# The first image of a convolution and attention kernel: channels normalised half by half, tables loaded later

## The chip, the cores and the metric

The kernel runs on one core of a Trainium2 chip. The metric is the device time of one execution in microseconds (us); lower is better. A kernel's time is the median of its runs.

## What is computed

The reference takes an image batch x of shape (2, 256, 56, 56) through a convolutional layer and one layer of two parts behind it. What matters here is the first layer, and in front of it a normalisation over groups of eight channels:

```
x = group_norm(x)                        # groups of 8 channels, per image
y = einsum('oc,bchw->bohw', w_qkv1, x)   # 256 -> 768 channels
y = depthwise_conv3x3(y, w_qkv2)         # 9 taps per channel
q, k, v = y.reshape(B, H, W, 3, 8, 32)   # a reshape of the flat array
for s in (0, 1):                         # two neighbourhood attentions, 7 x 7, dilation 1 and 2
    attn = softmax(q k + bias table of rpb[s]);  out = attn v
o = einsum('oc,bchw->bohw', w_proj, out)
```

Then a linear attention with a feed-forward part and a mixture of eight experts with two chosen per token follow. Everything is in 32-bit floats.

## The kernel before, in words

**Start.** The class `Convolutions` (L419) loads the whole image x_sb as [128, 2, 3136]: the 256 channels are two halves of 128 partitions (ct = 0 and 1). `load_x` (L462) issues four transfers for each half, ct 0 on SyncE's queue and ct 1 on ScalarE's. Then come g8 (the matrix that averages over eight channels), w2 (the taps), wq1 (the 256 x 768 weights, on SyncE's queue). `norm_image` (L469) takes 14 statistics on VectorE (seven chunks of 448 columns, two halves), two aggregates, a matmul with g8 for the mean, four small operations, a matmul for the variance, a power on GpSimd, and then scales x_sb in place in six operations, both halves in turn, chunk by chunk. Which instruction comes first on an engine is decided by a scheduler from the order of the program and from priorities; `tc.issue_after(x)` holds an instruction behind another one, `tc.high_priority()` moves it ahead, and `tc.manual_schedule(engines=...)` keeps the written order on those engines.

**Convolution.** `run` (L504) goes over two images, six blocks of 128 output channels (oc) and two strips of 28 rows (hf). For each strip, four groups of rows (8, 8, 8 and 5) are multiplied (L529, two channel halves accumulated in one PSUM bank, two banks in turn), copied by ScalarE into the padded strip ypad (L535), and put through nine taps: TensorE does the first 8 rows with diagonal matrices (L550), which GpSimd makes from w2 (diag, L519); ScalarE does the first tap of the other 20 rows (yc, L569) and VectorE the other eight (L579). The strip is stored to HBM (yd, L587). There are two ypad strips and two yc buffers.

**Bias tables.** `bias_tables` (L363) builds for each of the two attentions a table of exponentials. pf is zeroed (L368) and written to HBM as frame (L371); the 676 values of rpb are written reversed, one by one, to turned in HBM (L374); turned is written into frame (L379), frame is read back into pf (L383). After the first two strips, ScalarE takes the exponential (L387), GpSimd multiplies with a column mask (cm, L405) and with the two columns of far (L407 to L409), and stores three tables fp per attention (L411). The attention loads table tiles from fp (L714).

**Queues.** SyncE issues nearly all transfers in its own order: x, weights, frame and turned, the stores of yd, the table tiles, and the loads of q, k and v from yd (L804, L863). An instruction that waits holds up what stands behind it. Eight semaphores serve the transfers of both queues in turn, so that a transfer waits for the eighth before it.

**Attention and later stages.** `first_image` (L1064) runs the convolution and the first image's attention side by side: `conv.run()` and `att.run()` are generators that are stepped in turn. `Attention` (L607) holds PSUM tiles s_ps (four banks) and po (two banks) and loads the projection weights wpr (L639) when it is made. In the linear part, `keys` (L267) reads the tokens t, normalises them, rescales them (L296) and adds the output bias b2 if it was given one (L300); for the first half of the tokens it was given none but for the shared block t_ab, and `message` (L1918) adds it on GpSimd (L1925).

Of the kernel before, what the change touches and what calls it, by code (L numbers as in the profile page):

```python
# [13 lines left out]
F32 = mybir.dt.float32  # L14
AF = mybir.ActivationFunctionType
ALU = mybir.AluOpType
# [4 lines left out]
P = 128  # L21
B, C, HH, WW = 2, 256, 56, 56
T = HH * WW
# [3 lines left out]
G = 448  # L27
NG = T // G
NA = -(-T // 128)
NH6 = (NA - 1) // 4  # L30
NH = 4
# [95 lines left out]
def hybrid_kernel(ctx: ExitStack, tc: tile.TileContext, a: dict, out: bass.AP):  # L127
    nc = tc.nc
# [138 lines left out]
    def keys(tk, wk, sm, ps, bank, w_k, b2, kx, acc, n0, n, p, first, last, eager):  # L267
# [27 lines left out]
        for k in range(n):  # L295
            nc.scalar.activation(  # L296
                t[:, k, :], t[:, k, :], AF.Identity, bias=up[:, 1, k : k + 1], scale=up[:, 0, k : k + 1]
            )
        if b2 is not None:
            nc.gpsimd.tensor_tensor(t, t, b2[p].unsqueeze(1).to_broadcast([rows, n, C]), ALU.add)  # L300
        yield
        kps = bank()[p]
        for k in range(n):
# [59 lines left out]
    def bias_tables(sp, ac, pp):  # L363

        held = []
        for s in range(2):
            pf = sp.tile([NH * 21, 33], F32, name=f"pf{s}", bufs=1)
            nc.vector.memset(pf, 0.0)  # L368
            rpb = a[f"L0_conv_rpb{s}"]
            frame = dram.tile([NH, 21, 33], F32, name=f"frame{s}")  # L370
            nc.sync.dma_start(frame.rearrange("h r c -> (h r) c"), pf)  # L371
            turned = dram.tile([NH * 13, 13], F32, name=f"turned{s}")
            with nc.allow_non_contiguous_dma(reason="676 values"):
                nc.sync.dma_start(  # L374
                    turned, bass.AP(rpb.tensor, rpb.offset + 12, [[13, NH * 13], [-1, 13], [1, 1]])
                )
            held.append((pf, frame, turned))
        for pf, frame, turned in held:
            nc.sync.dma_start(  # L379
                frame[:, 4:17, 10:23],  # L380
                bass.AP(turned.tensor, turned.offset + 156, [[169, NH], [-13, 13], [1, 13]]),
            )
            nc.sync.dma_start(pf, frame.rearrange("h r c -> (h r) c"))  # L383
        yield
        for s in range(2):
            nw, pf = wide[s], held[s][0]
            nc.scalar.activation(pf, pf, AF.Exp)  # L387
            far = sp.tile([NH * 21, 2], F32, name=f"far{s}", bufs=1)
            nc.sync.dma_start(far, a["c_far"])

            if s == 0:
                stage = [ac.tile([P, 2, 800], F32, name="acc1") for _ in range(2)]
            else:
                stage = [
                    pp.tile([TT, NH, 448], F32, name="p").rearrange("p h n -> p (h n)")
                    .rearrange("p (k n) -> p k n", k=2) for _ in range(2)
                ]
            cm, near, late, early = (
                stage[k // 2][: NH * 21, k % 2, : KC * nw].rearrange("p (c j) -> p c j", j=nw) for k in range(4)
            )  # L400
            nc.sync.dma_start(cm, a[f"c_cm{s}k"].rearrange("p (c j) -> p c j", j=nw))
            o = 0
            for j0, nj in cols_of[s]:
                seen = bass.AP(pf.tensor, pf.offset + j0, [pf.ap[0], [1, KC], [1, nj]])
                nc.gpsimd.tensor_tensor(cm[:, :, o : o + nj], cm[:, :, o : o + nj], seen, ALU.mult)  # L405
                o += nj
            nc.gpsimd.tensor_scalar(late, cm, far[:, 0:1], 1.0, ALU.mult, ALU.mult)  # L407
            nc.gpsimd.tensor_scalar(early, cm, far[:, 1:2], 1.0, ALU.mult, ALU.mult)
            nc.gpsimd.tensor_scalar(near, late, far[:, 1:2], 1.0, ALU.mult, ALU.mult)  # L409
            for f, t in zip(fp[s], (near, late, early)):  # L410
                nc.gpsimd.dma_start(  # L411
                    bass.AP(
                        f.tensor, f.offset + (KC - 1) * NH * 21 * nw,
                        [[nw, NH * 21], [-NH * 21 * nw, KC], [1, nw]],
                    ),
                    t,
                )

    class Convolutions:  # L419


        def __init__(self, ctx):
# [11 lines left out]
            for hf in range(2):  # L434
                nc.gpsimd.memset(self.ypads[hf][:, hf * (HH // 2 + 1), :], 0.0)
                nc.gpsimd.memset(self.ypads[hf][:, :, 0:1], 0.0)
                nc.gpsimd.memset(self.ypads[hf][:, :, WW + 1 : WW + 2], 0.0)
            self.load_x(0)
            self.g8 = self.cw.tile([P, P], F32, name="g8")
            nc.scalar.dma_start(self.g8, a["c_g8"])  # L440
            self.w2 = self.cw.tile([P, 6, 9], F32, name="w2")
            nc.scalar.dma_start(
                self.w2, a["L0_conv_w_qkv2"].rearrange("(oc p) one kh kw -> p oc (one kh kw)", p=P)
            )
            self.wq1 = self.cw.tile([P, 2, 3 * C], F32, name="wq1")
            nc.sync.dma_start(self.wq1, a["w_qkv1_t"].rearrange("(ct p) o -> p ct o", p=P))

        def share(self, ctx):

# [51 lines left out]
                        gm[:, ct : ct + 1], grs[:, ct : ct + 1], ALU.subtract, ALU.mult,  # L501
                    )

        def run(self):  # L504


            w2 = self.w2
            for _ in self.norm_image():
                pass
            yield 0, 0  # L510
            for b, oc in ((b, oc) for b in range(B) for oc in range(6)):
                diag = None
                for hf in range(2):
# [8 lines left out]

                    r0 = hf * HH // 2
                    ypad = self.ypads[hf]
                    q0 = r0 - hf
                    for g0, n in ((0, 8), (8, 8), (16, 8), (24, 5)):
                        py = self.bank([P, 8, WW], "py")
                        for ct in range(2):
                            nc.tensor.matmul(  # L529
                                py[:, :n, :], self.wq1[:, ct, oc * P : (oc + 1) * P],  # L530
                                self.x_sb[:, ct, (q0 + g0) * WW : (q0 + g0 + n) * WW],
                                start=(ct == 0), stop=(ct == 1),
                            )
                        k0 = 1 - hf + g0
                        anchors["copied"] = nc.scalar.copy(  # L535
                            ypad[:, k0 : k0 + n, 1 : WW + 1], py[:, :n, :]
                        ).ins
                        if not shared:
                            yield b, oc
# [67 lines left out]
    class Attention:  # L607
# [6 lines left out]
        def __init__(self, ctx, b, order, banks=None, spare=None):  # L614
# [8 lines left out]
            self.ps_s = ctx.enter_context(tc.tile_pool(name=f"p2ps{b}", bufs=1, space=PSUM, **kw))  # L623
            bp, op = self.pool["b"], self.pool["x"]
            self.wpr = op.tile([P, 2, C], F32, name="wpr", bufs=1)
            if not banks:
                self.load_projection()
            self.ones = op.tile([TT, HD], F32, name="ones2", bufs=1)
            nc.vector.memset(self.ones, 1.0)
            self.qT0 = bp.tile([P, HH, WW], F32, name="qT0")  # L630
# [433 lines left out]
    def first_image(conv, ph):  # L1064
# [2 lines left out]
        ctx = ExitStack()  # L1067
        att = Attention(ctx, 0, "l k b t p v r x ac")
        conv.share(ctx)
        run, steps = conv.run(), att.run()  # L1070
        need = next(steps)
        tables = bias_tables(conv.sp, att.pool["ac"], att.pool["p"])
        next(tables)
        for k, (b, done) in enumerate(run):
            if k == 5:
                with tc.issue_after(anchors["copied"]):
                    next(tables, None)
# [581 lines left out]
    def linear(ph, tk, half, behind=None):  # L1659
# [258 lines left out]
        def message(n0, n, qz, out):  # L1918
# [1 line left out]
            mns = []  # L1920
            ss = sm.tile([P, 4], F32, name="ssm")
            for k0 in range(0, n, 2):
                if half == 0:
                    tt = tk.at(n0 + k0, 2)
                    nc.gpsimd.tensor_tensor(tt, tt, b2.unsqueeze(1).to_broadcast([P, 2, C]), ALU.add)  # L1925
                pm = ps_h.tile([P, 2, C], F32, name="pm", tag="h")
                for k in range(min(2, n - k0)):
                    for b, c0, c1 in parts(n0, n):
# [204 lines left out]
        def all_keys():  # L2133
# [6 lines left out]
            for i in range(len(pairs) + 2):  # L2140
                for k in (1, 0, 2):
                    j = i - k
                    if j == i and j < len(pairs):
                        live[j] = keys(
                            tk, wk, sm, ps_a, bank, w_k, b2 if half or pairs[j][1] == 1 else None, kx, acc, *pairs[j], j == 0, j == len(pairs) - 1, j < 3 and half == 0
                        )
                    if 0 <= j < len(pairs):
                        next(live[j])
# [325 lines left out]
```

## Time and profile before

| | us |
|---|---|
| median of three runs | 1997.98 |
| lowest and highest run | 1995.13, 2001.15 |
| the profiled execution, its time | 1985.54 |
| its span in the trace | 1983.8 |
| first product matmul starts | 18.49 |
| first tap on VectorE starts | 28.41 |
| VectorE resumes after its longest stop of the first 100 us | 73.46 |

The profile shows one execution, which was faster than the runs that the median is of; durations in it are compared with its own time. The span is the time from the first to the last instruction, and 1.74 us lie around it. In a timeline, a line gives the start, the time covered, the engine (PE is TensorE, PEld its weight loads, DVE VectorE, ACT ScalarE, POOL GpSimd, SP SyncE; a q behind it is the engine's own queue), the line of the kernel, the operation, the tile written and the tile read, how often it runs in a row, and in brackets how long the engine was idle before it and what ended that. A line of waits names who waited and for whom, then the total in us, the number of waits and the longest. A matmul of 32-bit floats leaves two records.

### The profile page before, as it was taken

How to read it: one execution, taken by the hardware profiler on the slowest of the kernel's cores; microseconds unless marked ns; L12 is line 12 of the kernel's file. 1: busy time of each engine (PE TensorE's matmuls, PEld its weight loads, DVE VectorE, ACT ScalarE, POOL GpSimd, SP SyncE). 2: the span in 40 equal slices, each digit the busy share in tenths (PEclk: the TensorE clock that was granted, in tenths of full speed). 3: DMA queues.
4: the chain of work that ended last, by engine and by line, in shares of the span. 5: the costliest groups of instructions: out<-in, count | busy, mean ns of one | idle time of the engine just before them, and what ended most of it. 6: DMA issues, size and time to landing. Idle time of an engine off the chain costs nothing.

```text
span 1983.8 us, 27692 instructions
## 1 busy us (share of the span) xinstructions
PE 1840.1 (93%) x9996; PEld 1304.7 (66%) x9996; DVE 1093.3 (55%) x2728; ACT 705.8 (36%) x1337; POOL 578.8 (29%) x634
## 2 busy tenths in 40 slices
PE   6999899988989997999989989999999999999996
PEld 3444454556645564665668755668788888888885
DVE  6887988889888546555557434655622222222121
ACT  2233324334434223544536543323322222222332
POOL 4520042025202444111126311345422323222221
PEclk9999999999989996999999999999999999999998
DMA  4644422350003334754464210114677676767995
GB/s 113 152 114 128 152 75 84 101 151 35 25 33 94 107 85 140 205 153 137 130 191 126 72 35 32 46 62 133 182 227 198 185 201 186 200 190 197 299 279 166
DMA packets 200147, 268.79 MB, mean 135 GB/s; under 512 B 30952, under 2 KB 158614, under 8 KB 199760
## 3 DMA queue, kind: packets, MB, share of 16 engines
q1 hardware_dynamic: 167920, 223.95, 37.4%
q0 software_dynamic: 19728, 27.54, 7.4%
q10 hardware_dynamic: 12352, 15.43, 2.3%
q8 instruction: 81, 1.33, 0.3%
q14 instruction: 66, 0.54, 0.1%
HBM read 200.19 MB, written 70.95 MB: 137 GB/s over the span
## 4 chain that ended last, share of the span: by engine, by line
PE 48%; DMA 5%; DVE 3%; ACT 3%; issue 1%; SPq 0%; POOL 0%; ACTq 0%; DVEq 0%; POOLq 0%
PE ph L1617 13%; PE py L1637 13%; PE p L1961 4%; DMA xr<-xs 2%; PE x L1637 2%; PE py L1977 2%; PE x L1617 2%; DMA xs<-in_c_fill 2%; PE po L666 2%; PE pm L1931 1%; PE kx L317 1%; PE x L359 1%; PE kp L305 1%; PE pq L1888 1%; PE px L1584 1%; PE s_ps L652 1%
## 5 line engine op out<-in xcount | busy, mean ns | idle before, releaser
L1617 PE MATMUL ph<-xe,w1e 128*128 128x256 f32 (+1 forms) x1448 | 309.2, 369 | 10.6 <-ACT hT L1621 4.1
L1637 PE MATMUL py<-w2e,hT 128*128 128x256 f32 x1392 | 311.3, 379 | 0.0
L1621 ACT ACTIVATE hT<-ph,sv 128x256 f32<-128x256 f32 (+1 forms) x362 | 165.7, 462 | 387.3 <-PE ph L1617 384.2
L1617 PEld LDWEIGHTS ph<-xe,w1e 128*128 128x128 f32 x1448 | 261.2, 190 | 49.8 <-ACT hT L1621 6.1
L1637 PEld LDWEIGHTS py<-w2e,hT 128*128 128x128 f32 x1392 | 260.1, 190 | 33.1 <-issue 0.2
L168 POOL DMA_INDIRECT y<-yt,idi x101 | 160.2, 1587 | 322.6 <-DVE yt L1643 178.2
L579 DVE SCALAR_TENSOR_TENSOR yc<-ypad,w,yc 128x1120 f32<-128x1120 f32 x144 | 202.5, 1410 | 31.4 <-ACT yc L569 29.0
L262 POOL TENSOR_TENSOR rs<-rs,mhalf 128x2 f32<-128x2 f32 (+3 forms) x90 | 72.8, 812 | 325.4 <-DVE rs L261 277.6
L529 PE MATMUL py<-x_sb,wq 128*128 128x448 f32 (+1 forms) x384 | 155.9, 538 | 8.3 <-ACT ypad L535 4.4
L656 ACT ACTIVATE p<-s_ps 112x952 f32<-112x952 f32 (+5 forms) x88 | 102.1, 1160 | 150.6 <-PE s_ps L652 101.4
L1574 DVE CAST idi<-xr 128x2 int32<-128x2 f32 (+1 forms) x53 | 10.9, 205 | 255.9 <-DMA xr<-xs 255.9
L657 DVE TENSOR_TENSOR p<-p,tab 112x952 f32<-112x952 f32 (+5 forms) x88 | 122.0, 1389 | 47.4 <-ACT p L656 47.3
L550 PE MATMUL pc<-ypad,diag 128*128 128x448 f32 x324 | 131.4, 547 | 0.0
L1643 DVE SCALAR_TENSOR_TENSOR yt<-py,eq,yt 128x256 f32<-128x256 f32 x87 | 41.7, 482 | 156.3 <-PE py L1637 156.1
L1599 POOL TENSOR_SCALAR yt<-b2e,eq 128x256 f32<-128x256 f32 x101 | 50.7, 507 | 257.6 <-DMA b2e<-in_L_ffn_b 198.6
L529 PEld LDWEIGHTS py<-x_sb,wq 128*128 128x128 f32 x384 | 72.2, 199 | 71.4 <-issue 55.7
L168 POOL DMA_INDIRECT xs<-row,si x98 | 97.5, 995 | 64.4 <-DVE si L2108 34.7
L572 DVE SCALAR_TENSOR_TENSOR yc<-ypad,w,yc 128x784 f32<-128x784 f32 x96 | 104.9, 1114 | 1.3 <-ACT yc L569 0.9
L666 PE MATMUL po<-p,v 98*32 98x170 f32 (+5 forms) x960 | 70.8, 376 | 28.6 <-DVE p L657 15.3
L550 PEld LDWEIGHTS pc<-ypad,diag 128*128 128x128 f32 x324 | 60.0, 191 | 52.3 <-issue 48.5
L1961 PE MATMUL p<-xT,fw 128*128 128x512 f32 (+1 forms) x208 | 93.6, 573 | 0.0
L1961 PE MATMUL p<-m2T,fw 128*128 128x512 f32 (+2 forms) x224 | 93.4, 539 | 0.0
(394 smaller groups left out, 2883.8 us busy)
## 6 DMA issues: line engine op xcount, KB each, us to landing
w1e<-in_L_ffn_W SPq DMA_DIRECT2D x53, 1024.0 KB
w2e<-in_L_ffn_W SPq DMA_DIRECT2D x53, 1024.0 KB
yd<-yc SPq DMA_DIRECT2D x24, 784.0 KB
ld<-yd SPq DMA_DIRECT2D x28, 448.0 KB
xr<-xs SPq DMA_DIRECT2D x48, 260.0 KB
b2e<-in_L_ffn_b SPq DMA_DIRECT2D x53, 128.0 KB
t<-td SPq DMA_DIRECT2D x12, 512.0 KB
y<-t ACTq DMA_DIRECT2D x24, 256.0 KB
```

What stands on the lines that cost most here:

```text
L168: ins = nc.gpsimd.indirect_dma_start(out=dst[:, :], out_offset=bass.IndirectOffsetOnAxis(ap=index, axis=0), in_=src, in_offset=None, **kw,)
L529: nc.tensor.matmul(py[:, :n, :], self.wq1[:, ct, oc * P : (oc + 1) * P], self.x_sb[:, ct, (q0 + g0) * WW : (q0 + g0 + n) * WW], start=(ct ...
L550: nc.tensor.matmul(pc, diag[:, tap, :], ypad[:, dy : dy + SHARE, dx : dx + WW], start=(tap == 0), stop=(tap == 8),)
L572: nc.vector.scalar_tensor_tensor(yc[:, y0:y1, :], src, w, yc[:, y0:y1, :], ALU.mult, ALU.add)
L579: nc.vector.scalar_tensor_tensor(yc[:, y0:y1, :], src, w, yc[:, y0:y1, :], ALU.mult, ALU.add)
L656: nc.scalar.activation(p[:nk, :, :n], s_ps[:nk, :, :n], AF.Exp)
L657: nc.vector.tensor_tensor(grid(p), grid(p), table[:nk], ALU.mult)
L666: nc.tensor.matmul(dst[hs] if w is None else den[hs], v[:nk, hs] if w is None else w[:nk, :], p[:, h, :, o : o + q.shape[2]], start=first ...
L1617: nc.tensor.matmul(p1, x.w1[:, ct, j * P : (j + 1) * P], x.xe[:, ct, :], start=(ct == 0), stop=(ct == 1),)
L1621: newest[3] = nc.scalar.activation(hT[:, j, :], p1, AF.Gelu, bias=x.sv[:, 4 + j : 5 + j]).ins
L1637: nc.tensor.matmul(py, hT[:, j, h * P : (h + 1) * P], x.w2[:, j, :], start=(j == 0), stop=(j == NJ - 1),)
L1961: nc.tensor.matmul(p1[:, :w], fw1[:, k, oc * P : (oc + 1) * P], rhs, start=(k == 0), stop=(k == 3))
```

## The change

The first image's start is written out by hand in a new function. The transfers of x come half by half, each half on both queues, with g8 and the first 128 columns of wq1 between them; the rest of wq1 comes on ScalarE's queue after w2. VectorE and TensorE follow the written order: statistics, mean, variance and scaling of the first half, with products of the first half, then the same for the second. Six groups are multiplied ahead (the four of the first strip and two of the second) into the attention's PSUM tiles s_ps and po; the loop of the convolution takes them from `self.ready`. The second image still uses `norm_image`.

The bias tables are begun after that in the program; the memsets of pf are held behind the second half's second statistic, and turned, far, the column masks and the projection weights are held behind the first write of frame. In `keys` the output bias is always given, and the adds in `message` are gone.

```diff
-        if b2 is not None:
-            nc.gpsimd.tensor_tensor(t, t, b2[p].unsqueeze(1).to_broadcast([rows, n, C]), ALU.add)
+        nc.gpsimd.tensor_tensor(t, t, b2[p].unsqueeze(1).to_broadcast([rows, n, C]), ALU.add)
...
-            nc.vector.memset(pf, 0.0)
+            with tc.issue_after(anchors["counted"]), tc.high_priority():
+                nc.vector.memset(pf, 0.0)
             rpb = a[f"L0_conv_rpb{s}"]
             frame = dram.tile([NH, 21, 33], F32, name=f"frame{s}")
-            nc.sync.dma_start(frame.rearrange("h r c -> (h r) c"), pf)
+            ld = nc.sync.dma_start(frame.rearrange("h r c -> (h r) c"), pf)
+            anchors.setdefault("framed", ld.ins)
             turned = dram.tile([NH * 13, 13], F32, name=f"turned{s}")
-            with nc.allow_non_contiguous_dma(reason="676 values"):
+            with tc.issue_after(anchors["framed"]), nc.allow_non_contiguous_dma(reason="676 values"):
                 nc.sync.dma_start(
...
-            nc.sync.dma_start(far, a["c_far"])
+            with tc.issue_after(anchors["framed"]):
+                nc.sync.dma_start(far, a["c_far"])
...
-            self.load_x(0)
             self.g8 = self.cw.tile([P, P], F32, name="g8")
-            nc.scalar.dma_start(self.g8, a["c_g8"])
+            self.wq1 = self.cw.tile([P, 2, 3 * C], F32, name="wq1")
+            wq1 = a["w_qkv1_t"].rearrange("(ct p) o -> p ct o", p=P)
+            for ct in range(2):
+                for k, (c0, c1) in enumerate(zip((0, G, 3 * G, 5 * G), (G, 3 * G, 5 * G, T))):
+                    eng = nc.scalar if k % 2 else nc.sync
+                    eng.dma_start(self.x_sb[:, ct, c0:c1], xv[0, :, ct, c0:c1])
+                if ct == 0:
+                    nc.scalar.dma_start(self.g8, a["c_g8"])
+                    nc.sync.dma_start(self.wq1[:, :, :P], wq1[:, :, :P])
...
-            nc.sync.dma_start(self.wq1, a["w_qkv1_t"].rearrange("(ct p) o -> p ct o", p=P))
+            nc.scalar.dma_start(self.wq1[:, :, P:], wq1[:, :, P:])
...
+        def first_block(self, att):
...
+            def count(ct, *gs):
+                for g in gs:
+                    ins = nc.vector.bn_stats(st[:, ct, g, :], x_sb[:, ct, g * G : (g + 1) * G]).ins
+                    if (ct, g) == (1, 1):
+                        anchors["counted"] = ins
...
+            with tc.manual_schedule(engines={mybir.EngineType.PE, mybir.EngineType.DVE}):
+                count(0, *range(NG))
+                mean(0)
+                variance(0)
+                count(1, 0)
+                scaled(0, 0, G)
+                products(0, 0)
+                count(1, 1)
+                scaled(0, G, T // 2)
+                products(0, 1)
+                count(1, *range(2, NG))
+                mean(1)
+                scaled(0, T // 2, T)
+                products(0, 2)
+                variance(1)
+                products(0, 3, 4, 5)
+                scaled(1, 0, G)
+                products(1, 0)
+                scaled(1, G, T // 2)
+                products(1, 1, 2)
+                scaled(1, T // 2, T)
+                products(1, 3, 4, 5)
+            self.ready = {r[:2]: d for r, d in zip(rows, places)}
...
-                        py = self.bank([P, 8, WW], "py")
-                        for ct in range(2):
-                            nc.tensor.matmul(
...
+                        py = self.ready.pop((hf, g0), None)
+                        if py is None:
+                            py = self.bank([P, 8, WW], "py")
+                            for ct in range(2):
+                                self.product(py, oc, hf, g0, n, ct)
...
-        next(tables)
         for k, (b, done) in enumerate(run):
+            if k == 0:
+                next(tables)
+                with tc.issue_after(anchors["framed"]):
+                    att.load_projection()
...
-                if half == 0:
-                    tt = tk.at(n0 + k0, 2)
-                    nc.gpsimd.tensor_tensor(tt, tt, b2.unsqueeze(1).to_broadcast([P, 2, C]), ALU.add)
```

`mean(ct)` issues the aggregate, the matmul with g8 and four small operations on VectorE; `variance(ct)` the second matmul, an addition on VectorE and the power on GpSimd; `scaled` one scaling of the given columns; `products(ct, *ks)` one matmul for each of the groups ks.

## The prediction

> **What bounds the kernel now.** I read the page's totals and its 40 slices first, to see which engine sets the pace and where it doesn't.
>
> ```profile
> span 1983.8 us, 27692 instructions
> ...
> PE 1840.1 (93%) x9996; PEld 1304.7 (66%) x9996; DVE 1093.3 (55%) x2728; ACT 705.8 (36%) x1337; POOL 578.8 (29%) x634
> ...
> PE   6999899988989997999989989999999999999996
> ...
> DMA  4644422350003334754464210114677676767995
> ```
>
> TensorE is busy 93% of the span; of its slices (49.6 us each) only the first and the last are at 6 tenths. The change rewrites the first, so next I read the timeline of the start.
>
> ```profile
> 14.86 0.59 PE L486 MATMUL gps<-mv,g 128*128 128x2 f32 x2 [14.86 <-DVE mv L480]
> ...
> 17.92 4.50 DVE L499 TENSOR_SCALAR x_sb<-x_sb,gm,rs_gn 128x448 f32<-128x448 f32 x6 [0.85 <-POOL rs_gn L151]
> ...
> 18.49 8.14 PE L529 MATMUL py<-x_sb,wq 128*128 128x448 f32 x16 [1.62 <-DVE x_sb L499]
> ...
> 23.14 0.32 PEld L529 LDWEIGHTS py<-x_sb,wq 128*128 128x128 f32 x1 [0.41 <-issue]
> ...
> 24.39 0.19 PEld L529 LDWEIGHTS py<-x_sb,wq 128*128 128x128 f32 x1 [0.18 <-issue]
> ...
> 26.46 6.94 PE L550 MATMUL pc<-ypad,diag 128*128 128x448 f32 x18
> ```
>
> No product runs before 18.49; then a matmul is two records, 0.75 us apart until 23.6 and 0.375 us after it (starts of the weight loads). But the start is not what the next stage waits for. VectorE's timeline, the waits of 28 to 74 us, and SyncE's timeline show that:
>
> ```profile
> 28.41 11.33 DVE L579 SCALAR_TENSOR_TENSOR yc<-ypad,w,yc 128x1120 f32<-128x1120 f32 x8 [5.99 <-ACT yc L569]
> 40.69 27.36 DVE L579 SCALAR_TENSOR_TENSOR yc<-ypad,w,yc 128x1120 f32<-128x1120 f32 x16 [0.95 <-ACT yc L569]
> 73.46 1.49 DVE L579 SCALAR_TENSOR_TENSOR yc<-ypad,w,yc 128x1120 f32<-128x1120 f32 x1 [5.42 <-ACT yc L569]
> ```
>
> ```profile
> ACT yc L569 <- DMA yd<-yc: 8.5, 1, 8.5
> ```
>
> ```profile
> 9.45 0.40 SPq L371 DMA_DIRECT2D frame<-pf  x1
> 9.89 1.03 SPq L374 DMA_DIRECT2D turned<-in_L_conv_rpb  x1
> ...
> 12.11 0.82 SPq L374 DMA_DIRECT2D turned<-in_L_conv_rpb  x1
> ...
> 24.75 7.86 SPq L379 DMA_DIRECT2D frame<-turned  x2
> ...
> 33.60 2.38 SPq L383 DMA_DIRECT2D pf<-frame  x2
> ...
> 58.15 1.75 SPq L714 DMA_DIRECT2D tab<-fp  x2
> 59.99 0.81 SPq L587 DMA_DIRECT2D yd<-yc  x1
> ...
> 72.17 0.84 SPq L804 DMA_DIRECT2D ld<-yd  x2
> ```
>
> VectorE stops at 68.04 and stands 5.42 us until 73.46, because ScalarE waits 8.5 us for a store of yc to free its buffer. That store was issued at 59.99, behind the table loads at 58.15, which had waited 17.9 us (SyncE's waits) for the tables. So a **chain of small transfers** decides when the stage goes on: turned (landed 24.75 and, from the second L379, 32.0), frame, pf, the exponentials on ScalarE at 39.18, GpSimd's products from 39.50, fp, then the store. VectorE has 5.42 us of slack behind it, TensorE 2.3 us (its wait at 73.89).
>
> **The change, part by part.** What stands where on an engine is read from the order of the two built programs.
>
> *Output bias.* Before, 12 adds `t<-t,b` (L1925) of 1.27 us run on GpSimd at 435.8 to 500.3. In the changed program they stand in the very same places of GpSimd's order; only the line that issues them differs. Cost 0.
>
> *First half of the channels ahead.* The transfers moved 1.4 MB by 6.0 us and 3.2 MB by 10.4, and the last wait for x ended at 11.10, 0.7 later. The first half (1.6 MB, with 0.2 MB of g8 and weights among it) lands at about 7.7. The last two of seven statistics (0.57 each) end at 9.0, the aggregate (0.27) at 9.3. From aggregate to first scaling took 3.1 us (14.81 to 17.92): scaling of the first half starts at 12.4 instead of 17.92, and its products follow.
>
> *But VectorE runs in written order.* Before the second half's mean stand a scaling of 448 (0.51), one statistic (0.57), two memsets (0.13), a scaling of 1120 (0.86), five statistics (2.85) and the aggregate: 5.2 us, to 17.6. The mean's matmul and four small operations (1.42) give 19.0, the scaling of 1568 that stands next (1.09) 20.1, the variance and the power (1.2) 21.3. So the second half is scaled from **21.3 instead of 17.92**, and done at 23.8.
>
> *TensorE.* Ahead of the first second-half product stand the last three of the first half, from 20.1: 2.0 us at 0.375 a record, 3.9 at 0.75. The fourth group needs the last scaling (23.8), so the first four groups are complete at 24.9 to 26.7; I take 25.7 (before: 26.46). Two more groups are complete at 27.2. Before, the second strip's products began only at 33.24 and took 5.3; now 1.7 us of them are left after the nine taps (27.6 + 6.94 = 34.5), so the last copy ends at 37.0 and ScalarE is free for the exponentials then, not at 39.18: **-2.2 us**.
>
> The clock bounds this from the other side. The records halve after 4.9 us of unbroken products, and in the new order the early products have a pause: two groups, at 12.9 and 14.5, take 1.5 each to 16.0, and the next waits for the mean's matmul at 17.6. If all twelve second-half records stayed at 0.75, they would take 4.2 longer (ten times 0.375, two of 280 columns 0.23 each): 37.0 becomes 41, and -2.2 becomes +2. I take the fast record, since products run without a break from 20.1.
>
> [...]
>
> *ScalarE.* The four copies of the first strip now wait once, for the whole tile s_ps: 25.9, three of 0.53 and 0.39, one of the second strip 0.53, then yc (1.23), done at 29.6. VectorE's taps start at 29.6 instead of 28.41: +1.2, covered by its 5.42 of slack.
>
> *Interleaved taps, an added wait.* VectorE's new order does six taps of the first strip and then the first of the second, whose yc stands on ScalarE behind both exponentials. Queued behind it are two taps of the first strip, its store, and all later taps.
>
> *Tables later.* frame is written after memsets that now stand after the ninth statistic (13.65), so the first turned is issued at 14.2 (before 9.89) and the second at 15.5 (12.11). No trace shows it in a free queue. Bounds: the second lands 19.9 us after issue as before (35.4); or no earlier than two spacings of 7.25 after 16.3 (30.8). Before, both stood behind wq and wpr, which were through at about 13.5 (4.3 MB moved); they now start about 1 us after that, so I take 33.0 (before 32.0). pf for the first table follows as before by 3.1 (36.1), for the second by 6.5, one more small load (0.5) than before (39.5).
>
> *Sum.* The first exponential needs pf 36.1 and ScalarE 37.0: 37.0, so the GpSimd chain starts 2.2 us earlier and the store with it, 57.8 instead of 59.99. The second waits until 39.5, so the second strip's yc is ready at 41.0, VectorE idles from 37.9 to 41.0 and has 18 taps left: 27.36 for 16 and two of 1.39 give 71.2, against 71.3 from the store chain. The two chains meet; the stage resumes near 71.5, **about -2 us**. With turned at 35.4 the taps end at 73.7: +0.2.
>
> *Weights.* The rest of wq (640 columns) is needed at about 36, w2 at 21.5, and the projection only after the first bands: cost 0. If w2 landed later than 21.4, GpSimd's diag would start later and the nine taps on TensorE with it, one for one. One memset of acc (0.83) passes behind the first power on GpSimd, which idles there: 0.
>
> *Other order.* Up to about 345 us the taps, scores and copies stand in another order; after that all orders agree. From 72 to 320 us TensorE is idle 22.7 us and VectorE 41. The new order can win or lose part of that; nothing in the profile gives the sign. I take 0 and keep a quarter of TensorE's idle time, 6 us, on both sides, and 0.5 of loss in the sum for the early taps' contention with GpSimd (taps were 1.39 us alone, 1.67 beside it).
>
> Sum: -2 + 0.5 = **-1.5 us**: profiled execution 1985.54 to 1984.0, span 1982.3. That execution is 12.4 us below the median of the runs shown, so the median goes from 1997.98 to **1996.5**.
>
> **Rivals.**
> (a) *The start passes through, and the order gains.* If the first copies come at 24 and the tables keep up, the most that the chain gives is 2.2; with 6 from the order, 1990. For it: idle time is there to win. Against it: the store chain caps the start's gain.
> (b) *Slower: the tables' late start.* Place: frame behind the memsets. turned later than 39 makes pf for the second table 45.5, VectorE's second strip 47, and the end of its taps 77, which is 4 us behind today's restart at 73.46; with the order's 6 against it, 2008. It decides from a landing of the second turned at 35.4 on. For it: 14.9 and 19.9 us from issue to landing. Against it: a freer queue.
> (c) *It doesn't do what it says.* The second half's scaling at 21.3 is late enough that the products run no earlier: 1998 to 1999.
>
> **Numbers.** A measurement tells 0.3%, 6 us, from no change. Forecast with (c), within 6 us: 0.56. (a), faster than 1992: 0.24. (b), and an unlucky order, slower than 2004: 0.20. The range 1987 to 2007 takes in the chain's bounds (-2.2 to +4) and most of the order's 6 and of the 6 us over which the shown runs spread. Chances: faster 0.24, same 0.56, slower 0.20.
>
> **What would show it.** Right: first product near 12.9, second half scaled near 21, four copies in one burst near 26, exponentials near 37 and 39.5 with ScalarE waiting for pf between, VectorE standing still after six taps, the store of the second strip near 58, VectorE resuming near 71.5. Wrong: turned landing before 25 or after 39; products still at 0.75 after 24; VectorE not waiting for the store at all; the spans apart only after 100 us, which would mean that the order decides.

## The result, and the profile after

The changed kernel takes 1995.57 us (median of 20 runs, 1988.9 to 2001.23), the kernel before, run beside it, 1997.44 (20 runs, 1990.7 to 2004.94): ratio 0.9988, 95% interval 0.9979 to 0.9998. Two later comparisons of the same two kernels gave 1.001 (0.9994 to 1.0026) and 0.9995 (0.9978 to 1.0011). Over the three nothing is left that this measurement tells from no change. The profiled execution took 1995.36 us. It is 9.8 us longer than the profiled execution of before, although the median is not: the two profiles can be compared stage by stage, but not by their ends.

The page of the changed kernel: span, busy totals, and the rows of TensorE and of the transfers in 40 slices.

```profile
span 1993.6 us, 27712 instructions
...
PE 1839.1 (92%) x10000; PEld 1303.2 (65%) x10000; DVE 1095.9 (55%) x2733; ACT 706.2 (35%) x1337; POOL 575.0 (29%) x635
...
PE   7899898978999997899989989999999999999996
...
DMA  4754422350014234664464210113677676767995
```

The totals are the old ones. The first slice of TensorE went from 6 to 7 tenths; other slices differ by a tenth to either side. TensorE's timeline of the start shows what filled the first:

```profile
13.89 3.35 PE L583 MATMUL s_ps<-x_sb,wq 128*128 128x448 f32 x4 [1.96 <-DVE x_sb L549]
...
21.78 3.19 PE L583 MATMUL po<-x_sb,wq 128*128 128x448 f32 x4
24.77 3.07 PE L583 MATMUL s_ps<-x_sb,wq 128*128 128x448 f32 x8
```

Products run from 13.89. But the four records that start at 21.78 cover 3.19 us, so they are still 0.75 apart, and the eight that start at 24.77 cover 3.07: the fast record (0.375) comes only from 25.3 on. ScalarE's timeline:

```profile
27.88 1.70 ACT L615 COPY ypad<-s_ps 128x448 f32<-128x448 f32 x4 [18.29 <-PE s_ps L583]
...
39.02 0.35 ACT L388 ACTIVATE pf<-pf 84x33 f32<-84x33 f32 x2
```

The four copies come in one burst, as the wait for the whole tile makes them, and the exponentials start at 39.02 (before 39.18). VectorE's timeline:

```profile
31.17 8.49 DVE L659 SCALAR_TENSOR_TENSOR yc<-ypad,w,yc 128x1120 f32<-128x1120 f32 x6 [7.07 <-ACT yc L649]
40.52 30.28 DVE L659 SCALAR_TENSOR_TENSOR yc<-ypad,w,yc 128x1120 f32<-128x1120 f32 x18 [0.87 <-ACT yc L649]
74.22 2.98 DVE L659 SCALAR_TENSOR_TENSOR yc<-ypad,w,yc 128x1120 f32<-128x1120 f32 x2 [3.42 <-ACT yc L649]
```

The three lines stand for six taps, a short stop for the second strip's yc, 18 taps, and a stop of 3.42 us until 74.22. SyncE's timeline, and the waits of SyncE and of ScalarE between 28 and 74 us, show what ended that stop:

```profile
16.57 0.83 SPq L375 DMA_DIRECT2D turned<-in_L_conv_rpb  x1
...
32.93 0.60 SPq L380 DMA_DIRECT2D frame<-turned  x1
...
58.30 1.74 SPq L792 DMA_DIRECT2D tab<-fp  x2
60.93 0.37 SPq L667 DMA_DIRECT2D yd<-yc  x1
...
72.92 0.84 SPq L882 DMA_DIRECT2D ld<-yd  x2
```

```profile
SPq L667 <- DVE yc L659: 10.7, 2, 9.9
```

```profile
ACT yc L649 <- DMA yd<-yc: 9.4, 1, 9.4
```

The second turned landed at 32.93, 16.4 us after its issue. The second strip's store goes out at 60.93. It no longer stands behind the table loads: it waited 9.9 us for VectorE, whose last tap of that strip comes late in the interleaved order. It then takes 12.0 us until ScalarE may use its buffer again, and ScalarE waits 9.4 of them.

### The profile page after: what moved, and what is told of

It is laid out like the page before. It is cut to its first block, busy times and chain, and to the rows that moved or that the text cites. A ratio compares the mean times of both kernels' runs of the same rounds, so it can differ in the third digit from the quotient of the medians.

```text
span 1993.6 us, 27712 instructions
## 1 busy us (share of the span) xinstructions
PE 1839.1 (92%) x10000; PEld 1303.2 (65%) x10000; DVE 1095.9 (55%) x2733; ACT 706.2 (35%) x1337; POOL 575.0 (29%) x635
## 4 chain that ended last, share of the span: by engine, by line
PE 51%; DVE 3%; ACT 2%; DMA 2%; issue 1%; POOL 0%; SPq 0%; ACTq 0%; POOLq 0%; DVEq 0%
PE py L1718 14%; PE ph L1698 14%; PE p L2039 4%; PE x L1718 2%; PE py L2055 2%; PE x L1698 2%; PE po L744 2%; PE pm L2009 1%; PE kx L316 1%; PE x L358 1%; PE kp L304 1%; DMA xr<-xs 1%; PE px L1665 1%; PE s_ps L730 1%; PE pq L1969 1%
## 5 line engine op out<-in xcount | busy, mean ns | idle before, releaser
L1698 PE MATMUL ph<-xe,w1e 128*128 128x256 f32 (+1 forms) x1448 | 310.8, 370 | 11.8 <-issue 3.4
L1655 DVE CAST idi<-xr 128x2 int32<-128x2 f32 (+1 forms) x53 | 10.3, 195 | 256.4 <-DMA xr<-xs 256.4
L583 PE MATMUL py<-x_sb,wq 128*128 128x448 f32 (+1 forms) x360 | 142.2, 525 | 9.4 <-ACT ypad L615 6.1
L583 PEld LDWEIGHTS py<-x_sb,wq 128*128 128x128 f32 x360 | 65.5, 193 | 67.6 <-issue 49.1
L744 PE MATMUL po<-p,v 98*32 98x170 f32 (+5 forms) x960 | 71.7, 375 | 29.3 <-issue 12.4
L2055 PE MATMUL py<-fw,hTl 128*128 128x264 f32 x392 | 91.8, 391 | 1.3 <-ACT hTl L2042 1.1
```

What stands on the lines that cost most here:

```text
L583: nc.tensor.matmul(py[:, :n, :], self.wq1[:, ct, oc * P : (oc + 1) * P], self.x_sb[:, ct, q0 * WW : (q0 + n) * WW], start=(ct == 0), stop= ...
L744: nc.tensor.matmul(dst[hs] if w is None else den[hs], v[:nk, hs] if w is None else w[:nk, :], p[:, h, :, o : o + q.shape[2]], start=first ...
L1698: nc.tensor.matmul(p1, x.w1[:, ct, j * P : (j + 1) * P], x.xe[:, ct, :], start=(ct == 0), stop=(ct == 1),)
L2055: nc.tensor.matmul(py[:, : C + E], hT[:, kk, c0 : c0 + P], fw2[:, kk, :], start=(kk == 0), stop=(kk == 3),)
```

## The experiments

The prediction's theory was that a chain of small transfers ending in this store decides when the stage goes on, so that the start has slack. Rivals: the start passes through to the end; the new order of taps and scores after the start decides; the lateness of the tables decides. This table puts all profiles side by side; each row's first four numbers come from one profile, the last two from all its runs. "First tap" is VectorE's first tap; "store" is the issue of the second strip's store less that of GpSimd's first store of the second attention's tables (fp<-p); "landing" is the time from the store's issue to the load of yd that waits for it; "stop" is VectorE's idle time between 65 and 77 us. "At equal clock" is the difference in time from the kernel before of the same comparison, in us, after taking out the mean granted clock of each run: one fit over 246 runs with a level for each kernel of each comparison, and one slope, which came out at -1.0 us for each 0.001 of clock; two standard errors are 1.7 us, or 2.3 for the two kernels with six runs. The fit takes it that an edit does not itself change the clock, which no run shows; by plain means, without the clock, the three kernels with more statistics stand at +6.8, +11.8 and +5.0 instead of +5.3, +14.5 and +4.7. (For the first comparison only the times of the kernel before were kept, so the field is empty.)

| kernel | first tap | store | landing | stop | ratio (95%) | at equal clock |
|---|---|---|---|---|---|---|
| before | 28.41 | +1.69 | 12.2 | 5.42 | | |
| before + bias edit | 28.39 | -0.06 | 5.6 | 0 | 0.9996 (0.9982, 1.001) | 0.0 |
| before, store first | 27.44 | -3.75 | 8.5 | 0 | 0.9999 (0.9985, 1.0014) | -0.1 |
| before, 7 statistics more | 32.87 | -0.13 | 6.2 | 0 | 1.0041 (1.002, 1.0062) | +5.3 |
| before, 21 more | 42.12 | +0.07 | 5.7 | 0 | 1.0064 (1.0039, 1.0088) | +14.5 |
| after, four groups ahead | 29.53 | -0.84 | 6.1 | 0 | 1.0003 (0.9987, 1.0018) | -0.1 |
| after, none ahead | 30.84 | -0.37 | 6.6 | 0 | 0.9999 (0.9982, 1.0016) | +2.5 |
| after | 31.17 | +2.69 | 12.0 | 3.42 | 0.9988 (0.9979, 0.9998) | |
| after, second time | 30.15 | +2.69 | 10.6 | 1.97 | 1.001 (0.9994, 1.0026) | +1.3 |
| after, third time | 30.28 | +2.69 | 10.3 | 1.74 | 0.9995 (0.9978, 1.0011) | +0.1 |
| after, tables early | 30.02 | +2.70 | 9.8 | 1.21 | 1.0003 (0.999, 1.0016) | +1.2 |
| after, matmuls in front | 32.88 | +2.69 | 10.3 | 1.75 | 1.0009 (0.9991, 1.0028) | +1.6 |
| after, 7 statistics more | 34.03 | +2.69 | 10.4 | 1.85 | 1.0021 (1.0007, 1.0036) | +4.7 |
| after, fp<-p late | 39.88 | -18.2 | 6.8 | 0 | 1.0043 (1.0028, 1.0059) | +6.2 |

**Four groups ahead.** Only the first strip is multiplied ahead; from there on the taps stand in the old order.

```diff
-                for k in ks:
+                for k in (k for k in ks if k < 4):
...
-            self.ready = {r[:2]: d for r, d in zip(rows, places)}
+            self.ready = {r[:2]: d for r, d in zip(rows[:4], places)}
```

> Only the four groups of the first strip are multiplied ahead instead of six; loads, normalisation and late tables as in the changed kernel. From the second strip on, every engine's order is again that of the kernel before. Order theory (the gain comes from the other order of 175 to 345 us): no gain, ratio 1.000 (0.999 to 1.0015), the second image's first yc near where the kernel before has it and the first of the second-half adds of bias near 436 us. Start theory (the early loads and products bring it): the gain stays, ratio 0.9988, and those adds near 432.

1.0003, against 0.9988 to 1.001 for the changed kernel with its new order: no difference between the two orders can be measured. VectorE does not stop near 70 us, though nothing was done to the store. That was the first sign against the store chain.

**The start made later**, in the new order and in the old one. The kernels take seven more statistics (some 4 us of VectorE), of chunks counted before, with the same values.

```diff
-                count(1, *range(2, NG))
+                count(1, *range(2, NG), *range(2, NG), 6, 6)
```

> The changed kernel with seven more statistics on VectorE (0.57 us each, 4.0 in all; chunks counted again, same values) before the second half's mean; every other engine's order is that of the changed kernel. If the start is on the path: 4 us more than the changed kernel, ratio to the kernel before about 1.0008. If slack behind the start hides it: ratio 0.9988 as the changed kernel.

The first tap came 3.8 us later than in the kernel's own repeats, and the time is 0.21%, 4.2 us, above the kernel before (+4.7 at equal clock, where the repeats have +1.3 and +0.1). Nothing of it was absorbed that the measurement could show.

```diff
+            if extra:
+                for g in [6] * 7:
+                    nc.vector.bn_stats(st[:, 1, g, :], x_sb[:, 1, g * G : (g + 1) * G])
             for ct in range(2):
```

> The kernel before with seven more statistics (4.0 us) before its aggregates; all orders else unchanged. If the start is on the path through ScalarE's exponentials (39.18) and the chain of tables: VectorE resumes at 77.5 instead of 73.5, the bias adds start near 440 instead of 436, ratio 1.002. If the start has slack: 73.5, 436, ratio 1.000.

First tap 4.5 us later, time 5.3 us longer at equal clock. The slack of 5.42 us that the profile of before showed behind the first tap did not take it up.

**Tables early.** The memsets of pf are no longer held, the table transfers are not held behind the first write of frame, and the tables are begun before the loop. The products ahead stay.

```diff
-            with tc.issue_after(anchors["counted"]), tc.high_priority():
-                nc.vector.memset(pf, 0.0)
+            nc.vector.memset(pf, 0.0)
...
+        next(tables)
         for k, (b, done) in enumerate(run):
             if k == 0:
-                next(tables)
```

> The changed kernel, with the memsets of pf at the very start and no hold on the tables' transfers; orders of all engines else as in the changed kernel. If the late tables cost time, this is faster than the changed kernel by 1 to 2 us (ratio 0.998). If ScalarE's own place for the exponentials (39.0) decides, turned lands several us earlier and nothing else moves: ratio 0.9988, VectorE resumes at 74.2.

turned went out at 7.31 and 9.01 instead of 14.87 and 16.57, and pf was issued by 30.86 instead of 36.78. The exponentials still started at 37.88, against 38.01 and 38.13 in the repeats of the changed kernel: ScalarE's last copy decides there, and the late tables cost nothing that can be measured.

**The kernel again, the bias edit alone, no products ahead, store first.** The second is the kernel before with only the output bias moved to `keys`; all engines keep the order of before. The third does the changed start without its products.

> The changed kernel once more, beside the others on one chip. If the first comparison (0.9988) holds: 0.9988 again. If the new order alone, as tables_early has it (1.0003), brings nothing: 1.000. Second look at the stage: the first add of bias at 432 (as in its first profile) within 2 us.

1.001: the 0.12% of the first comparison did not come back. VectorE's stop is 1.97 us, where the first profile had 3.42.

```diff
-        if b2 is not None:
-            nc.gpsimd.tensor_tensor(t, t, b2[p].unsqueeze(1).to_broadcast([rows, n, C]), ALU.add)
+        nc.gpsimd.tensor_tensor(t, t, b2[p].unsqueeze(1).to_broadcast([rows, n, C]), ALU.add)
...
-                if half == 0:
-                    tt = tk.at(n0 + k0, 2)
-                    nc.gpsimd.tensor_tensor(tt, tt, b2.unsqueeze(1).to_broadcast([P, 2, C]), ALU.add)
```

> The kernel before with only the bias edit; the order of every engine is the same as before. Both theories: ratio 1.000 (0.999 to 1.001). It is also a second profile of the order of before: if the 12 us that the second strip's store took there belong to that order, VectorE resumes near 73.5 again and the bias adds start near 436; if they were chance, the store takes about 6 us as in slow_before and ahead4, VectorE hardly stops, and the adds start near 428 to 432.

0.9996. Its use lies elsewhere: it gives a second profile of the order of before. VectorE's and SyncE's timelines of this kernel:

```profile
40.67 35.88 DVE L578 SCALAR_TENSOR_TENSOR yc<-ypad,w,yc 128x1120 f32<-128x1120 f32 x22 [0.95 <-ACT yc L568]
```

```profile
56.39 1.75 SPq L713 DMA_DIRECT2D tab<-fp  x2
58.23 0.56 SPq L586 DMA_DIRECT2D yd<-yc  x1
...
63.87 1.81 SPq L803 DMA_DIRECT2D ld<-yd  x2
```

After its eight first taps VectorE runs on through 22 taps, to the end of this view, without the stop at 68 us. The store went out at 58.23, 1.8 us earlier than in the profile of before, because the first attention's tables had landed 1.8 us earlier (table loads at 56.39 against 58.15). But its data were through 5.6 us after issue, not 12.2: the buffer came free 8.3 us earlier. So the stop of before, and with it the slack that the prediction used, does not belong to the order: one profile of it has the stop and the other has not.

```diff
                 for k in ks:
-                    self.product(places[k], 0, *rows[k], ct)
+                    pass
...
-            self.ready = {r[:2]: d for r, d in zip(rows, places)}
+            self.ready = {}
```

> The changed kernel's loads, half-by-half normalisation and late tables, but no product ahead: the first products wait for both halves. From the first strip on, all orders are those of the kernel before. First product pair complete near 23 instead of 20, first tap on VectorE near 32 instead of 28.4. If a late start passes through as in slow_before (4.0 us of extra work, about 4.6 at equal clock): +3 to +4 us, ratio 1.0015 to 1.002. If slack hides it: 1.000.

0.9999. The first tap is only 0.7 us later than in the changed kernel's second run, so the six products ahead bring little by themselves. At equal clock the time is 2.5 us longer than that of before, for a first tap 2.4 us later: the plain ratio hides it, since the mean clock of these runs was higher (0.9742 against 0.9730).

```diff
-                with urgent():
+                with tc.issue_after(anchors["store", 0, 1]) if (s, r) == (0, 0) and not self.banks else urgent():
```

> The kernel before, with the first table tile's loads held behind the second strip's store on SyncE. If the store behind the tables is what stops VectorE: the store is issued near 54 instead of 60, VectorE's stop of 5.4 us shrinks below 2, and the bias adds start 3 to 5 us earlier, ratio 0.998. The order of the first image's attention changes with it, which may add or take 4 us. If the stop is harmless: ratio 1.000.

Here the kernel before loads its first table tiles after the second store (which also reorders the first image's attention). The store went out at 53.58, VectorE did not stop, and the time is 0.9999. With the stop taken away nothing is gained that can be measured; how many of the runs of before beside it had the stop is not known, since only profiles show it. The store took 8.5 us here, although it was 3.75 us ahead of the first fp<-p: the first store of the first attention's tables (fp<-acc, at 49.17) stood 4.4 us ahead of it.

**A third time, and fp<-p late.** The kernel was run unchanged once more:

> The changed kernel a third time, beside three others. Two comparisons gave 0.9988 (0.9979 to 0.9998) and 1.001 (0.9994 to 1.0026). If the difference is nothing that a measurement can tell: again within 0.9985 to 1.0015. The second strip's store, issued 2.7 us behind the first store of the second attention's tables, lands in 10 to 12 us as in its two profiles.

0.9995. Next, in the changed kernel, the second attention's tables are begun only at a later strip, behind a store of yd, so that no fp<-p stands ahead of the second strip's store.

```diff
+            if s == 0:
+                yield
...
+            if k == 9:
+                with tc.issue_after(anchors["store"]):
+                    next(tables, None)
```

> The changed kernel, with the second attention's table work (exponential, products, stores fp from p) held until later strips are stored. If the second strip's store is slow because it is issued behind those stores: it lands in about 6 us (5.6 to 6.6 in the four runs that issued it ahead of them) instead of 10 to 12, and VectorE's stop of 2 to 3.4 us near 70 is gone. If the store is slow for its own sake or for the table loads: 10 to 12 again. Total: ratio 0.998 if that stop was on the path, 1.000 if later waits take it up; the later order moves a little too.

The wait for the store is what it was meant to show. SyncE's timeline: the store, and the load of yd that waits for it,

```profile
66.64 0.46 SPq L669 DMA_DIRECT2D yd<-yc  x1
...
73.45 0.83 SPq L884 DMA_DIRECT2D ld<-yd  x2
```

6.8 us apart, and VectorE does not stop. The total says nothing about this stop, since the edit had a side effect. ScalarE's timeline has the first exponential ahead of the copies:

```profile
36.49 0.23 ACT L388 ACTIVATE pf<-pf 84x33 f32<-84x33 f32 x1 [27.31 <-DMA pf<-frame]
36.63 1.66 ACT L617 COPY ypad<-s_ps 128x448 f32<-128x448 f32 x4
```

It waited 27.31 us for pf, and the copies, whose groups were complete at about 26.3, queued behind it: the first tap comes at 39.88. This wait at the head of ScalarE's order made the start late. TensorE stood idle for 9.44 us until 37.29, and its granted clock was 0.50 from 32.76 to 43.0: its nine taps from 37.29 on took 9.84 us, where the kernel before needs 6.94. The 6.2 us of the table hold both, and no run separates them.

**21 statistics more**, otherwise as the seven: is there any slack at all?

> The kernel before with 21 more statistics (12 us) before its aggregates, all other orders unchanged. If a late start passes through whole: 12 us more, ratio 1.006, the first add of bias near 443. If waits of the first 200 us take up 4 us of it, as slow_before's profile had it: 8 us, 1.004, near 439. If the stage has all that slack: 1.000, 431.

No: the first tap is 13.7 us late and the time 14.5 us longer at equal clock (12.3 by the medians).

**Matmuls in front.** In the changed kernel 48 matmuls of the identity into a bank that is written again later stand ahead of the first mean, to see whether TensorE's record can be made fast earlier.

```diff
+            def warm(n):
+                for _ in range(n):
+                    nc.tensor.matmul(po[:, 1, :P], ident, ident, start=True, stop=True)
...
+                warm(48)
                 count(0, *range(NG))
```

> The changed kernel with 48 small matmuls of ident by ident ahead of the first mean (results overwritten), to keep TensorE at work from 2 us on; all later orders as in the changed kernel but for their places in TensorE's list. If the early products are slow because TensorE had no unbroken work: records at 0.375 us from the first product or from 20 us on, the four groups complete near 26 instead of 27.7, exponentials near 37.5 instead of 39, stage 1 to 2 us earlier, ratio to before 0.999. If the slow records have another cause: no change in any of it.

It was badly sized, since the 96 records ended only at about 14, behind which the first mean had to wait. TensorE's timeline still answers the question:

```profile
1.51 12.64 PE L530 MATMUL po<-ident 128*128 128x128 f32 x96 [1.51 <-POOL ident masks.py:199]
...
16.93 1.02 PE L588 MATMUL s_ps<-x_sb,wq 128*128 128x448 f32 x2 [1.45 <-DVE x_sb L553]
18.29 1.53 PE L588 MATMUL s_ps<-x_sb,wq 128*128 128x448 f32 x2 [0.34 <-DVE x_sb L553]
...
21.76 1.84 PE L588 MATMUL s_ps<-x_sb,wq 128*128 128x448 f32 x2
```

The first two product records cover 1.02 us, the next two 1.53, and after another pause, of 1.5 us, two cover 1.84, as without the matmuls in front. The fast record came back at 25.5. The granted clock in three stretches of this trace (its share of full speed is the number behind POOL's) says the same:

```profile
15.25:18.66 3.41, 1.62 (x5) 0.74 (x6) 2.99 (x8) 0.00 (x0) 0.57 (x1) 1.00 0.04 8
18.70:25.40 6.70, 5.21 (x11) 2.73 (x10) 5.04 (x14) 0.00 (x0) 1.31 (x3) 0.50 0.44 30
25.50:40.00 14.50, 14.50 (x41) 7.50 (x40) 8.57 (x8) 4.75 (x9) 6.72 (x16) 1.00 0.23 30
```

In each line stand the stretch, its length, the busy time of PE, PEld, DVE, ACT and POOL, the clock, and what the transfers did. The clock was full up to 18.66, and half after a stretch of 3.41 us in which TensorE was busy for 1.62. So the record was fast ahead of the products that matter (0.51 us at 16.9), and slow again when they ran (0.92 at 21.8).

## Why the prediction was right in its number and wrong in a step

**The number.** 1996.5 was forecast and 1995.57 measured; "within 0.3%" was right, and so was that no part of the change is worth more than a few us. That the two numbers agree to 0.9 us is luck: the three comparisons lie between 0.12% faster and 0.10% slower, and the -1.5 was not confirmed.

**Right.** The first half's scaling (12.82; forecast 12.4), the second half's (21.64; 21.3) and its end (24.1; 23.8); the second turned landing (32.93; 33.0); the bias adds, which cost 0 (the edit alone: 0.9996); the order, priced at 0 (four groups ahead: 1.0003); the weights. Rival (b), the tables' late start, is out: with early tables the time is 1.0003. VectorE's short stop after six taps is 0.87 us, not 3.1, because both pf were there before ScalarE was free.

**Mis-sized: TensorE's record.** I took 0.375 us from 20.1 on, because products run without a break there. The profiled execution changed over at 25.3; the repeats, the early tables and the four groups at 23.4 to 23.7, the very moment of before (23.6). In both repeats TensorE was fast for a while behind the early products (a pair of weight loads took 0.30 us from 18.0 to 19.7, 0.50 before) and slow again from 20.2 or 20.4 on. The second run's granted clock shows it:

```profile
16.75:20.10 3.35, 1.77 (x7) 0.82 (x6) 2.74 (x9) 0.00 (x0) 0.00 (x0) 1.00 0.41 31
20.20:23.50 3.30, 3.27 (x5) 1.85 (x6) 2.49 (x4) 0.00 (x0) 3.18 (x5) 0.50 0.57 35
23.60:40.00 16.40, 16.40 (x47) 8.60 (x46) 8.80 (x7) 6.50 (x13) 6.53 (x17) 1.00 0.17 30
```

TensorE was fast from 16.73 to 20.14, but busy for only 1.77 us of that, and slow again for the next 3.41 us, in which the last three products of the first half lie. The profile of before can't show the clock of its start: the first clock record of that trace begins at 23.39, just where the matmuls' records became short, and for 0 to 20 us, where it has none, a view prints 1.00 too. The exponentials moved by -0.2 us in the first profile and by -1.2 and -1.05 in the repeats, not by -2.2. The bound of +2, all records slow, was on the right side.

When the clock changes over is told by the traces only so far. In those of before and of the changed kernel's first run, every stretch of granted clock but the last is a whole number of 3.41 us. The two stretches of full clock shown here, with matmuls in front and in the second run, held 1.62 and 1.77 us of TensorE work in their last 3.41 us, with no pause above 1.5, and half clock followed both. The changeover of one kernel is not fixed: 25.3, 23.6 and 23.7 us in the three profiles of the changed kernel. How much work brings the full clock, or keeps it, no run shows; that unbroken products from 20.1 on would was the author's estimate.

**The step that failed: "the start is not what the next stage waits for".** I read VectorE's 5.42 us stop in one execution as slack of the kernel. Two things fell.

First, the stop is the outcome of a race. In 13 of the table's 14 profiles, a store issued at most 0.1 us after the first fp<-p landed within 5.6 to 6.8 us, and one issued 1.69 us or more after it took 9.8 to 12.2; the 14th, store first, was ahead of fp<-p but 4.4 us behind the first fp<-acc, and took 8.5. In the old order store and fp<-p come almost together; before lost by 1.69 us, the same order in the bias edit won by 0.06. In the new order the store waits for the interleaved taps and lost by 2.69 or 2.70 us in all six profiles that keep it, so there VectorE stops for 1.2 to 3.4 us each time. Here the prediction's path was wrong as well: in the repeats the table loads went out at 56.32 and 56.09, the 2 us earlier that the chain promised, but the store only at 59.90 and 60.03 instead of 57.8. That VectorE resumed at 71.75 and 71.64, as forecast (71.5), is luck. The kernel with fp<-p moved away is the counter-check: without the fp<-p ahead the stop is gone. Why a store that is only 2 us later needs twice as long is not shown. That rows of fp are under way beside it can't be all of it: with the bias edit the store went out 0.06 us ahead of the first of three fp<-p, whose median to landing was 12.0 us, and was through in 5.6.

Second, the start counts, and no cost of the race can be measured. Where the start isn't delayed on purpose, kernels with the stop and kernels without it lie within 0.12% of before. The first tap, on the other hand, is paid: 4.5 us late gave +5.3 at equal clock, 13.7 gave +14.5, in the new order 5.6 gave +4.7. So the +1.2 us of VectorE's later taps, which I had "covered by its 5.42 of slack", is a cost: it measured +1.7 to +1.9 in the repeats (2.8 in the first profile). Against it stand the earlier exponentials (-1.1). An estimate from these two, if both count in full, is +0.7 us, in place of my -1.5; the two comparisons with equal clock give +1.3 and +0.1, each within 1.7. Both signs of so small a sum lie inside what can be measured, which is why the forecast held although a step of it was wrong.

**Open.** The landmark behind the stage, the first bias add on GpSimd, came at 428.3 us with no products ahead, at 431.6 with the bias edit and also in before with seven statistics more, and at 435.8 in before. In these single profiles a start up to 4.5 us late has vanished by then, while the run times say that it is paid. The clock explains part of it: up to the landmark TensorE ran at half clock for 20.5 us with the bias edit, but for only 13.7 in before with seven statistics more and in the kernel with no products ahead. The 6.8 us of difference are worth at most 3.4 us, an estimate from half the speed (a record of 0.75 us against 0.375). The landmark of one order varies by 4.2 us from profile to profile (before had 23.9 us at half clock), so I trust the times; the rest isn't settled. Matmuls in front (first tap 4.5 late, +1.6) and fp<-p late (11.5 late, +6.2) were paid less than in full. Why is not shown: the changed kernel with seven statistics more has the same products ahead, and there 4.7 of 5.6 us were paid.

## What to carry to other kernels

A wait in one profile is slack only if it is there in a second profile of the same order: take one, or delay the suspected path by a known few us and see whether the time follows. Work pulled ahead of a bottleneck gains only the part by which the next reader starts earlier; here ScalarE waited for all four groups at once, and VectorE, the next in line, started later than before (30.15 to 31.17 against 28.41). And a store that is made to wait for later work may meet other traffic that it used to pass: here it went out 2.69 us behind the first fp<-p and took 10.3 to 12.0 us.

## What the runs showed of the hardware

- **A store of a strip beside stores of a table.** The second strip's store (784 KB, from its issue to the load that waits for it) took 5.6 to 6.8 us when issued ahead of GpSimd's three stores fp<-p (156.2 KB each) or at most 0.1 us behind the first, and 9.8 to 12.2 when issued 1.7 to 2.7 us behind it. Issued 3.75 us ahead of them, but 4.4 us behind the first of the other table's stores (fp<-acc, 248.1 KB each), it took 8.5.
- **TensorE's clock around a partly busy stretch.** With matmuls in front it was 1.00 up to 18.66 us and 0.50 up to 25.49, after 3.41 us with 1.62 of work and no pause above 1.5; a record took 0.51, 0.77 and 0.92 us at 16.9, 18.3 and 21.8. In the traces of before and of the changed kernel's first run the clock takes only the values 1.00 and 0.50, in stretches of whole multiples of 3.41 us but for the last.
- **Transfers of single values.** The two turned transfers landed 12.9 and 16.4 us after issue in the first profile of the changed kernel, 9.6 and 15.7 with fp<-p late, 9.9 and 15.6 with matmuls in front, 14.9 and 19.9 in before; issued 4.5 us later than in before, the second landed only 0.9 us later in that first profile.
- **Run time and clock.** The times of the changed kernel's 20 runs spread over 12 us. Over all 246 runs they follow the mean granted clock of the run, which lay between 0.964 and 0.980 (0.968 and 0.975 in those 20): 1.0 us less for each 0.001. Taking the clock out reduced the spread of single runs about their kernel's mean from 3.5 to 2.5 us (standard deviation).
